# Whole-sum rows placed inside layer 0's end and between the sort's steps, and layer 0's roots by logarithm and exponential

## The chip, the core and the metric

The kernel runs on one core of a Trainium2 chip. The metric is the device time of one execution, in microseconds; lower is better. The core has five engines, each with its own queue that it works off in order: PE (TensorE, matrix products), DVE (VectorE), ACT (ScalarE), POOL (GpSimd) and SP (which here only issues transfers).

## What is computed

Four layers work on 2708 nodes with 128 features and one dense 2708 x 2708 adjacency matrix. Each has the form `x = layernorm(x + layer(x, adj))`. The change lies in layer 0's end and layer 1's beginning:

```python
# layer 0
A_hat = A + eye;  d = A_hat.sum(axis=1) ** -0.5
x = layernorm(x + (d[:, None] * A_hat * d[None, :]) @ x @ W.T + b)
# layer 1
XW = x @ W
s_col, s_row = XW @ a[0, :f], XW @ a[0, f:]
den = exp(leaky_relu(s_row[:, None] + s_col[None, :], 0.01))
num = A @ den
att = where(num != 0, den / num, 0)
x = layernorm(x + A @ (att @ XW))
```

where `layernorm(v) = (v - mean) / sqrt(var + 1e-5)`. Layers 2 and 3 (a hyperbolic layer, and one that works on the signs of the adjacency) follow and are not touched.

## The kernel before

The features lie as 128 partitions by nodes. The nodes are cut into 22 tiles of 128 (`NT`) and into six blocks of 512 columns (`NB`; the last has 148 columns). An adjacency tile `(d, c)` holds row block d and column block c, four tiles of rows by 512 columns.

**Layer 0's end.** The column blocks are finished one after the other. For a block c, `last_products` does the rest of its matrix products on PE, `summed_up` adds input and bias on DVE and squares on ACT, `norm_roots` sums the squares over the features on PE (`group_sums`, the tile `var`), takes the root on ACT, the reciprocal on DVE, and splits the result into three bf16 terms (`three_terms`, on DVE). `normed` spreads these terms over the partitions on PE (`group_spread`, the tile `rs`) and multiplies on DVE, which gives `x`. `projected` multiplies by layer 1's weights on PE, and ACT copies the outcome to `xw` and `rc` (the two scores of each node). `clamped` limits the scores (`rcl`, DVE), and `count` compares each tile of scores with 384 sample values (DVE; 44 instructions in all). The steps of neighbouring blocks are interleaved by hand. The last two blocks, 4 and 5, have no products of later blocks beside them.

**The sort.** Layer 1 needs no matrix of all pairs: the leaky exponential is a maximum of two products, so the kernel sorts the nodes by their scores into 26 groups (`GM`) and works group by group. The steps are a chain between PE and DVE: `below` (PE sums the counts), `jp` and `prev` (DVE), `prev_ps` (three transposes on PE), `prev_row` (DVE), then 26 dependent steps `jk` on DVE (L1228), each of which finds the next group's begin. Then come one-hot tables `c`, `oh`, `val` (DVE and POOL), `low` (78 small products and four larger ones on PE, L1283 and L1293, that give each node its place in its group), `pos`, `slot`, `ohs` (DVE) and two lists, `list0` and `list1` (22 products each, L1335), each read back and worked on by DVE. From the lists come the addresses of gathered adjacency rows (`row_i`, list0) and of gathered weights (`xw_i`, list1), and the exponentials `e1_l`, `e2_l`, `gj_l`. `group_matrix` (the tile `gb`) builds the first three groups' weights from `gj_l`.

**The whole sums.** The first group's numerator needs the sum of `e1 * A` over all nodes. `whole_sum(n)` does the next n of 22 rows of it (one row is one tile of 128 nodes): nine products with one output row each, on four strips of the array (L797). The rows go through the row blocks in the order 0, 4, 5, 1, 2, 3. They read adjacency tiles `kept`; those of row blocks 0 to 3 are loaded once more (the tiles B, and one in `ut`) into places that become free. When a row block's last row has been recorded, `fetch_next` records the loads into the places that it frees, in SP's queue. The finished sums are copied by ACT to `carry0` (nine copies, L1380), which lies in `xw`'s memory.

**What sets the order.** A scheduler orders the instructions of each engine by their readiness. A helper overrides it: what is recorded under `queued(ENGINE)` is issued on that engine after the last thing so recorded (`latest`), in the order of the source. Outside of it, `tc.issue_after(instruction)` sets a single edge. Before the change, the rows stand as 4 before the sort, 1 after `prev_ps`, 6 between the transposes `rb`, 3 behind them, 4 after `low`, and 4 after the last product of `list1`.

After the sort the program reads a flag and branches. In the branch POOL gathers the groups' adjacency rows (L1417), and PE starts with two `gb` and then `num` (L1461). The gathered tiles take the memory of the tiles that the whole sums read.

## Time and profile before

| | |
|---|---|
| median of 3 runs | 933.85 us (931.97 to 933.93) |
| the profiled execution | 931.1 us, of which the span from first to last instruction is 929.4 us |
| PE, DVE, ACT, POOL busy | 92%, 61%, 40%, 16% of the span |
| granted clock of TensorE, mean | 0.97 |
| layer 0's end (blocks 0 to 3) | about 124 to 163.5 us |
| its tail (blocks 4 and 5) | about 163.5 to 177 us |
| sort and lists | about 177 to 236 us |
| first `num` product in the branch | 243.77 us |

Times are microseconds from the first instruction. PE's busy share is high over the whole kernel, but it is a mean over stages: in the tail PE was busy for 4.79 of 13.5 us. So the stretch that is changed has to be read by itself, by what each engine waits for. A busy PE at half its clock also counts as busy; the clock column of the windows tells the two apart.

### The profile page before, as it was taken

The numbers are of one execution on the slowest core, as the hardware profiler recorded it, in microseconds if no ns is written. First come the engines' busy times: TensorE is split into PE (matmuls) and PEld (weight loads), VectorE is DVE, ScalarE is ACT, GpSimd is POOL, SyncE is SP. The second block draws the span as 40 slices with busy tenths as digits, with TensorE's granted clock in tenths as the row PEclk, the third lists the DMA queues.
The fourth block names the chain that finished last, engine by engine and source line by source line (L and its number), as shares of the span: only waits on it lengthen the run. The fifth ranks groups of instructions, "written<-read, shape, count | busy, mean of one in ns | idle before, by whom it ended". The sixth has DMA issues, their size and how long they took to land.

```text
span 929.4 us, 9409 instructions
## 1 busy us (share of the span) xinstructions
PE 856.4 (92%) x3268; PEld 428.0 (46%) x3268; DVE 564.3 (61%) x1221; ACT 369.6 (40%) x601; POOL 152.5 (16%) x182
## 2 busy tenths in 40 slices
PE   3799988579799999999999999989999999999997
PEld 2344534235344444444444444454344455555555
DVE  4895569898488888878786222637554464333222
ACT  3885332110677777566664111536332221000000
POOL 5321000303655554222110000000000000000000
PEclk9799999798799999999999999999999999999999
DMA  9997492195596555344431876477956293746410
GB/s 338 373 351 240 52 310 67 43 386 217 172 356 204 163 154 162 121 131 138 150 120 44 290 268 240 152 253 258 334 186 226 63 343 115 250 144 242 142 55 15
DMA packets 95834, 182.84 MB, mean 197 GB/s; under 512 B 6430, under 2 KB 23535, under 8 KB 95652
## 3 DMA queue, kind: packets, MB, share of 16 engines
q1 hardware_dynamic: 85556, 142.37, 44.5%
q0 software_dynamic: 8352, 37.76, 12.9%
q10 hardware_dynamic: 1872, 2.04, 0.6%
q8 instruction: 27, 0.44, 0.2%
q14 instruction: 27, 0.22, 0.1%
HBM read 179.33 MB, written 2.84 MB: 196 GB/s over the span
## 4 chain that ended last, share of the span: by engine, by line
PE 77%; DVE 14%; DMA 5%; ACT 2%; issue 2%; ACTq 0%; DVEq 0%
PE a L1518 21%; PE uacc L1426 14%; PE a L1797 11%; PE a L860 9%; PE num L1461 7%; PE a L1806 6%; DVE att L1474 4%; DMA A<-in_adjT_dram 4%; PE t L797 2%; DVE jk L1228 2%; DVE att L1455 2%; DMA cb<-in_adjT_dram 1%; PE pp L1755 1%; DVE counts L1041 1%; PE low L1293 1%
## 5 line engine op out<-in xcount | busy, mean ns | idle before, releaser
L1426 PE MATMUL uacc<-att,xw_g 128*128 128x512 f32 (+1 forms) x312 | 130.4, 554 | 8.9 <-DVE att L1474 8.2
L1466 ACT ACTIVATE ln<-num,inval,occ_l 128x512 f32<-128x512 f32 (+1 forms) x156 | 106.5, 722 | 65.7 <-DVE gat L1465 63.3
L1797 PE MATMUL a<-cb,ut 128*128 128x512 f32 (+2 forms) x264 | 124.8, 554 | 0.4 <-DMA cb<-in_adjT_dram 0.4
L1806 PE MATMUL a<-mask,node 128*128 128x512 f32 (+2 forms) x264 | 119.5, 534 | 0.0
L1461 PE MATMUL num<-gat,w_all 128*128 128x512 f32 (+1 forms) x276 | 114.1, 543 | 0.0
L1518 PE MATMUL a<-cb,q_b 128*128 128x512 f32 (+2 forms) x264 | 110.3, 555 | 1.7 <-DMA cb<-in_adjT_dram 1.7
L1518 PE MATMUL a<-cb,xw 128*128 128x512 f32 (+2 forms) x264 | 107.4, 550 | 0.0
L860 PE MATMUL a<-A,q_b 128*128 128x512 f32 (+2 forms) x264 | 105.8, 549 | 0.0
L1417 POOL DMA_INDIRECT gat<-in_adjT_dram,row_i x52 | 78.4, 1508 | 146.4 <-PE num L1461 79.4
L1426 PEld LDWEIGHTS uacc<-att,xw_g 128*128 128x128 f32 x312 | 55.8, 189 | 90.7 <-issue 50.0
L1465 DVE COPY gat<-num 2x512 f32<-2x512 f32 x150 | 86.0, 608 | 3.3 <-PE num L1461 3.1
L1474 DVE TENSOR_TENSOR att<-att,ln 128x1354 f32<-128x1354 f32 x52 | 81.1, 1560 | 9.6 <-ACT ln L1473 9.6
L1455 DVE TENSOR_SCALAR att<-q_b,gj_l 128x1354 f32<-128x1354 f32 x52 | 47.8, 921 | 37.8 <-PE uacc L1426 37.8
L1806 PEld LDWEIGHTS a<-mask,node 128*128 128x128 f32 (+1 forms) x264 | 47.7, 190 | 49.3 <-issue 47.5
L1461 PEld LDWEIGHTS num<-gat,w_all 128*128 128x128 f32 x276 | 51.2, 191 | 41.4 <-issue 22.7
L1473 ACT ACTIVATE ln<-ln 128x1354 f32<-128x1354 f32 x52 | 69.3, 1333 | 1.3
L1785 DVE TENSOR_SCALAR mask<-cb 128x3072 fp32r<-128x3072 f32 (+5 forms) x24 | 33.5, 1394 | 58.8 <-PE a L1806 58.6
L860 PEld LDWEIGHTS a<-A,q_b 128*128 128x128 f32 (+1 forms) x264 | 45.6, 190 | 47.9 <-issue 46.9
L1518 PEld LDWEIGHTS a<-cb,xw 128*128 128x128 f32 (+1 forms) x264 | 45.0, 190 | 46.3 <-issue 46.3
L1518 PEld LDWEIGHTS a<-cb,q_b 128*128 128x128 f32 (+1 forms) x264 | 44.6, 189 | 46.2 <-issue 42.3
L231 ACT ACTIVATE sq_l<-s 128x512 f32<-128x512 f32 (+1 forms) x11 | 6.6, 604 | 147.1 <-DVE s L1815 116.7
L1060 ACT ACTIVATE xw<-A 128x2048 f32<-128x2048 f32 (+3 forms) x36 | 57.0, 1583 | 8.2 <-issue 4.4
(446 smaller groups left out, 904.7 us busy)
## 6 DMA issues: line engine op xcount, KB each, us to landing
cb<-in_adjT_dram SPq DMA_DIRECT2D x15, 2816.0 KB
cb<-in_adjT_dram SPq DMA_DIRECT2D x15, 2560.0 KB
A<-in_adjT_dram SPq DMA_DIRECT2D x25, 1024.0 KB
B<-in_adjT_dram SPq DMA_DIRECT2D x18, 1024.0 KB
cb<-in_adjT_dram SPq DMA_DIRECT2D x3, 814.0 KB
cb<-in_adjT_dram SPq DMA_DIRECT2D x3, 740.0 KB
ut<-in_adjT_dram SPq DMA_DIRECT2D x2, 1024.0 KB
A<-in_adjT_dram SPq DMA_DIRECT2D x5, 296.0 KB
```

The lines of the kernel that those rows point to most:

```text
L860: nc.tensor.matmul(acc[c][:, :w], lhsT=z[:kw, k, :], rhs=t[:kw, i, :w], start=c not in begun, stop=(d == NB - 1 and k == NT - 1), skip_gro ...
L1417: return nc.gpsimd.indirect_dma_start(out=gat[g], out_offset=None, in_=adj_h, in_offset=bass.IndirectOffsetOnAxis(ap=row_i[:, h, g : g + 1 ...
L1426: nc.tensor.matmul(uacc[c][:, : cb - ca], lhsT=xw_g[:, g, :], rhs=att[:, ca:cb], start=(g == 0), stop=(g == GM - 1),)
L1455: nc.vector.tensor_scalar(att, q_b[:, h0 : h0 + HALF], gj_l[:, g : g + 1], 1.0, op0=ALU.mult, op1=ALU.max)
L1461: nc.tensor.matmul(num[:, : cb - ca], lhsT=(w_first if g < FIRST else w_all)[:, g, :], rhs=gat[g][:, ca:cb], start=True, stop=True)
L1465: nc.vector.tensor_copy(gat[g + 1][0:2, ca:cb], num[0:2, : cb - ca])
L1466: nc.scalar.activation(ln_n[:, ca:cb], num[:, : cb - ca], AF.Ln, scale=occ_l[:, g : g + 1], bias=inval[:, g : g + 1],)
L1473: nc.scalar.activation(ln_n, ln_n, AF.Exp, scale=-1.0)
L1474: nc.vector.tensor_mul(att, att, ln_n)
L1518: nc.tensor.matmul(acc[:, :w], lhsT=weights[:kw, k, :], rhs=pc[:kw, t, :w], start=(k == 0), stop=(k == NT - 1),)
L1797: nc.tensor.matmul(acc[:, :w], lhsT=edge[:ke, k, :], rhs=pc[:ke, t, :w], start=(k == 0), stop=False, skip_group_check=True,)
L1806: nc.tensor.matmul(acc[:, :w], lhsT=node[:kw, k, j, :], rhs=mask[:kw, t - ma, :w], start=False, stop=(k == NT - 1 and j == 1), skip_group_ ...
```

## The change

1. `norm_roots`: instead of Sqrt on ACT and a reciprocal on DVE, ACT takes the logarithm and then twice the exponential of -0.5 times it: once into bf16 (`term`, the first of the three terms) and once into fp32 (`r`). `three_terms` leaves out its first cast.
2. ACT's function table for Ln and Exp is loaded right behind the tanh of `prepare_rest`, and what is queued on ACT afterwards comes behind that load.
3. The exponentials `e1` are taken block by block in `clamped`.
4. The rows are recorded by `sum_rows` at new places: 1 after the roots of blocks 4 and 5, 1 between `normed` of block 4 and of block 5, 2 after `projected` of block 5, 3 between `below` and `prev_ps`, 6 between the `rb` as before, 3 behind them, 4 after `low` and the flag's product `gps`, and 2 ahead of `list1`. None stands behind `list1`. The products of `prev_ps`, `low`, `gps` and the lists are put into the fixed order of PE too.
5. The product of `oh` with the partition's number, twice 128 x 572 elements, moves from POOL to ACT.

```diff
--- before.py
+++ after.py
@@ -257,13 +257,14 @@
                 stop=True,
             )
 
-    def three_terms(two, r, rest, term):
+    def three_terms(two, r, rest, term, begun=False):
 
 
         n = r.shape[0]
         for i, dst in enumerate((rest, two)):
             src = rest if i else r
-            nc.vector.tensor_copy(term, src)
+            if i or not begun:
+                nc.vector.tensor_copy(term, src)
             nc.vector.scalar_tensor_tensor(dst, term, behind[:n, i : i + 1], src, op0=ALU.mult, op1=ALU.add)
 
     def group_spread(ps, two, b):
@@ -381,6 +382,8 @@
     bsum = const.tile([P, F], F32, tag="bsum", name="bsum")
     w2ext = const.tile([P, F + 1], F32, tag="w2ext", name="w2ext")
 
+    curved = []
+
     def prepare_rest():
 
         ysq = const.tile([P, F], F32, tag="ysq", name="ysq")
@@ -388,7 +391,7 @@
         nc.vector.tensor_reduce(y2, ysq, AX.X, ALU.add)
         bn = clipped_norm("bn", y2, 1)
         bt = c_tile("bt", 1)
-        nc.scalar.activation(bt, bn, AF.Tanh)
+        curved.append(nc.scalar.activation(bt, bn, AF.Tanh).ins)
         bs = multiplied("bs", divided("bq", bt, bn, 1), proj_scale("bp", bt, 1), 1)
         nc.vector.tensor_scalar(y, b2_s, bs, None, op0=ALU.mult)
         nc.vector.tensor_mul(ysq, y, y)
@@ -969,10 +972,12 @@
             r, rest = own[:, :P], own[:, P : 2 * P]
             term, two = (own[:, i * P : (i + 1) * P].bitcast(BF16)[:, :P] for i in (2, 3))
             with queued(ACT):
-                nc.scalar.activation(r, pv[:n, :P], AF.Sqrt, bias=eps_c[:n, :])
+
+                nc.scalar.activation(r, pv[:n, :P], AF.Ln, bias=eps_c[:n, :])
+                nc.scalar.activation(term, r, AF.Exp, scale=-0.5)
+                nc.scalar.activation(r, r, AF.Exp, scale=-0.5)
             with queued(DVE):
-                nc.vector.reciprocal(r, r)
-                three_terms(two, r, rest, term)
+                three_terms(two, r, rest, term, True)
             works[c, "r"] = two
 
         def normed(c):
@@ -1021,6 +1026,8 @@
                 if c == NB - 1:
                     for i in range(2):
                         nc.vector.tensor_add(cmp_v[:, i, span], cmp_v[:, i, span], pad_big[:, span])
+            with queued(ACT):
+                nc.scalar.activation(e1[:, span], rcl[:, 0, span], AF.Exp)
             if c == 0:
                 ps = ps_tile("samples_ps")
                 with queued(PE):
@@ -1047,6 +1054,10 @@
                         op1=ALU.add,
                         accum_out=counted[:, i, t + 1 : t + 2],
                     )
+
+        def sum_rows(n):
+            with queued(PE):
+                return whole_sum(n)
 
         scaled = None
 
@@ -1101,6 +1112,8 @@
                 prepare_finish()
         with tc.issue_after(scaled), tc.issue_after(rooted[0]):
             prepare_rest()
+        with tc.issue_after(curved[0]):
+            latest[ACT] = nc.scalar.preload_act_table_set("natural_log_exp_and_others").ins
         nc.sync.dma_start(out=diag_d, in_=bass.AP(tensor=adjT.tensor, offset=0, ap=[[N + 1, N], [1, 1]]))
 
         fetch_next()
@@ -1131,12 +1144,15 @@
         count(NB - 3, 1, 3)
         norm_roots(NB - 2)
         norm_roots(NB - 1)
+        sum_rows(1)
         count(NB - 3, 3, 6)
         normed(NB - 2)
+        sum_rows(1)
         normed(NB - 1)
         count(NB - 3, 6)
         projected(NB - 2)
         projected(NB - 1)
+        sum_rows(2)
         clamped(NB - 2)
         count(NB - 2)
         clamped(NB - 1)
@@ -1156,11 +1172,6 @@
 
 
         with queued(ACT):
-            nc.scalar.activation(e1[:, : tiles(1)[0]], rcl[:, 0, : tiles(1)[0]], AF.Exp)
-        with queued(PE):
-            whole_sum(4)
-        with queued(ACT):
-            nc.scalar.activation(e1[:, tiles(1)[0] :], rcl[:, 0, tiles(1)[0] :], AF.Exp)
             nc.scalar.activation(e2, rcl[:, 0, :], AF.Exp, scale=0.01)
 
         with tc.tile_pool(name="sort", bufs=1) as st_p:
@@ -1203,21 +1214,19 @@
                     )
             nc.vector.tensor_tensor(prev[:, 0, :], prev[:, 0, :], prev[:, 1, :], op=ALU.max)
             prev_ps = ps_tile("prev_ps")
-            for q in range(len(SAMPLES)):
-                turned = nc.tensor.transpose(
-                    prev_ps[:, q * P : (q + 1) * P], prev[:, 0, q : q + 1].to_broadcast([P, P]), ident
-                )
-            with tc.issue_after(turned.ins):
-                summed = whole_sum(1)
-            latest[PE] = summed.ins
+            sum_rows(3)
+            with queued(PE):
+                for q in range(len(SAMPLES)):
+                    nc.tensor.transpose(
+                        prev_ps[:, q * P : (q + 1) * P], prev[:, 0, q : q + 1].to_broadcast([P, P]), ident
+                    )
             for b in range(NB):
                 w, cs = width(b), bslice(b)
                 with queued(PE):
                     pr = bcast_block(rcl[:, 0, :], b, f"rb{b}")
                     whole_sum(1)
                 nc.scalar.activation(q_b[:, cs], pr[:, :w], AF.Exp, scale=0.99)
-            with queued(PE):
-                whole_sum(3)
+            sum_rows(3)
             prev_row = srt([P, NS], "prev_row", F16)
             nc.vector.tensor_copy(prev_row, prev_ps[:, :NS])
 
@@ -1274,32 +1283,31 @@
                 )
                 nc.vector.tensor_sub(oh[i], c3[i][:, :, :GM], c3[i][:, :, 1:])
                 nc.gpsimd.tensor_mul(val[i][:, :, 0, :], oh[i], tile_b.unsqueeze(2).to_broadcast(grid))
-                nc.gpsimd.tensor_scalar(val[i][:, :, 1, :], oh[i], part_f, None, op0=ALU.mult)
+                nc.scalar.activation(val[i][:, :, 1, :], oh[i], AF.Copy, scale=part_f)
             low = {}
             for i in range(2):
                 for h, (ta, tb) in enumerate(((0, t_a), (t_a, NT))):
                     low[i, h] = acc_tile(2 + 2 * i + h, f"low{i}_{ta}")
                     nn = (tb - ta) * GM
-                    nc.tensor.matmul(
-                        low[i, h][:, :nn],
-                        lhsT=upper,
-                        rhs=oh[i][:, ta:tb, :],
-                        start=True,
-                        stop=False,
-                        skip_group_check=True,
-                    )
-                    for t in range(tb - 1):
-                        first = max(t + 1, ta)
-                        placed = nc.tensor.matmul(
-                            low[i, h][:, (first - ta) * GM : nn],
-                            lhsT=ones_b,
-                            rhs=oh[i][:, t, :].unsqueeze(1).to_broadcast([P, tb - first, GM]),
-                            start=False,
-                            stop=(t == tb - 2),
+                    with queued(PE):
+                        nc.tensor.matmul(
+                            low[i, h][:, :nn],
+                            lhsT=upper,
+                            rhs=oh[i][:, ta:tb, :],
+                            start=True,
+                            stop=False,
                             skip_group_check=True,
                         )
-            with tc.issue_after(placed.ins):
-                summed = whole_sum(4)
+                        for t in range(tb - 1):
+                            first = max(t + 1, ta)
+                            nc.tensor.matmul(
+                                low[i, h][:, (first - ta) * GM : nn],
+                                lhsT=ones_b,
+                                rhs=oh[i][:, t, :].unsqueeze(1).to_broadcast([P, tb - first, GM]),
+                                start=False,
+                                stop=(t == tb - 2),
+                                skip_group_check=True,
+                            )
             below0 = srt([P, 1], "below0")
             okb = srt([P, 1], "okb")
             nc.vector.tensor_reduce(below0, neg_sum, AX.X, ALU.add)
@@ -1310,7 +1318,9 @@
             nc.vector.tensor_scalar(good, good, okb, None, op0=ALU.mult)
             nc.vector.tensor_reduce(gs, good, AX.X, ALU.add)
             gps = ps_tile("gps")
-            nc.tensor.matmul(gps[0:1, 0:1], lhsT=gs, rhs=ones[:, 0:1], start=True, stop=True)
+            with queued(PE):
+                nc.tensor.matmul(gps[0:1, 0:1], lhsT=gs, rhs=ones[:, 0:1], start=True, stop=True)
+            sum_rows(4)
             nc.vector.tensor_scalar(flag_i, gps[0:1, 0:1], float(N), None, op0=ALU.not_equal)
 
 
@@ -1328,11 +1338,13 @@
                 nc.vector.tensor_reduce(slot[:, i, :], pos[i], AX.X, ALU.add)
                 nc.vector.tensor_scalar(slot[:, i, :], slot[:, i, :], 2.0, None, op0=ALU.add)
                 ps = ps_tile(f"list{i}")
+                if i:
+                    sum_rows(2)
                 for t in range(NT):
                     ohs = srt([P, P], f"ohs{i}_{t}", BF16, 4, "ohs")
                     nc.vector.tensor_scalar(ohs, iota_b, slot[:, i, t : t + 1], None, op0=ALU.is_equal)
-                    with tc.issue_after(summed.ins):
-                        listed = nc.tensor.matmul(
+                    with queued(PE):
+                        nc.tensor.matmul(
                             ps[:, : 6 * GM],
                             lhsT=ohs,
                             rhs=val[i][:, t, :, :].rearrange("p n g -> p (n g)"),
@@ -1367,8 +1379,6 @@
                     nc.vector.tensor_copy(occ_l, occ)
 
                     nc.vector.tensor_scalar(inval, inval, 1.0e-18, None, op0=ALU.max)
-            with tc.issue_after(listed.ins):
-                whole_sum(4)
 
             nc.vector.tensor_scalar(sc, e1_l, -1.0, unit0[:, 0:1], op0=ALU.mult, op1=ALU.add)
             nc.vector.tensor_scalar(bi, e2_l, unit0[:, 1:2], None, op0=ALU.add)
```

On PE the same instructions stand in another order. On DVE 12 are gone (six reciprocals, six casts). On ACT two table loads go and one comes, and 12 Exp (two a block in place of each of the six roots' single Sqrt, which becomes Ln), six `e1` in place of two, and two copies. On POOL two instructions are gone. SP's queue has the same transfers in the same order.

## The prediction

> **What bounds the kernel now.** I read the chain of waits first (its stretch 160 to 245 us; the change touches nothing later), then the same stretch by windows, PE's waits, the groups and SP's queue. Chain rows are start, length, work:
>
> ```profile
> 177.02 6.72 PE t L797 x58
> 184.50 3.23 DVE jp L1195 x12
> 187.97 0.92 PE prev_ps L1207 x3
> 188.91 0.57 DVE prev_row L1222
> ...
> 216.01 4.61 PE t L797 x56
> ...
> 225.86 3.28 PE list L1335 x19
> 229.14 6.49 PE t L797 x50
> ```
>
> Three blocks of whole-sum rows (L797) lie in the open chain: 6.7, 4.6 and 6.5 us. Rows also run beside the 26 jk steps of DVE (189.5 to 206.6), where they cost nothing.
>
> ```profile
> 163.50:177.00 13.50, 4.79 (x31) 3.43 (x30) 11.93 (x43) 3.74 (x11) 3.36 (x9) 0.64 0.15 46
> 183.70:189.50 5.80, 2.13 (x16) 0.98 (x19) 4.26 (x16) 0.00 (x0) 0.00 (x0) 0.84 0.89 304
> 229.10:243.80 14.70, 8.00 (x79) 3.30 (x79) 3.82 (x18) 5.00 (x13) 6.45 (x5) 0.73 0.34 104
> ...
> 225.00:226.00 1.00, 0.28 (x2) 0.10 (x1) 1.00 (x11) 0.24 (x2) 0.00 (x0) 0.61 0.06 16
> 231.00:232.00 1.00, 1.00 (x8) 0.13 (x1) 0.00 (x0) 0.00 (x0) 0.00 (x0) 0.50 0.03 8
> ```
>
> Columns: length, busy PE, PEld, DVE, ACT, POOL, then granted clock, DMA share, GB/s. PE has idle time at layer 0's end (4.79 busy of 13.5), DVE not (11.93). The clock falls to half about 225.4, in the sparse list matmuls, and is back at 232.
>
> ```profile
> PE rs L273 <- DVE work L267: 8.7, 6, 2.5
> PE xw L993 <- DVE x L984: 1.8, 1, 1.8
> ...
> L972 ACT ACT_TABLE_LOAD x1 | 1.3, 1283 | 0.0
> ...
> L974 DVE RECIPROCAL work<-work 128x128 f32<-128x128 f32 (+1 forms) x6 | 5.7, 947 | 3.0 <-ACT work L972 3.0
> ...
> 183.34 23.06 SPq L818 DMA_DIRECT2D B<-in_adjT_dram  x12
> 206.49 2.12 SPq L818 DMA_DIRECT2D ut<-in_adjT_dram  x1
> 208.71 5.75 SPq L818 DMA_DIRECT2D B<-in_adjT_dram  x2
> ```
>
> PE waits 8.7 us for the roots' DVE chain. The B tiles' reloads are issued as rows finish and free places, and run at 386 GB/s until about 222.3.
>
> **The change part by part.** One row costs 1.18 us at full clock (four in 4.73 from 215.94), 2.38 at half (188.80 to 191.18).
>
> *Roots.* Before: Sqrt 0.37, 0.03 of handover, reciprocal 0.95, cast 0.26, first scalar_tensor_tensor: 1.61 from Sqrt's start. After: Ln 0.37, two Exp of 128x128. No such row: a 128x148 Square took 0.327, a 128x26 Exp 0.23, so 0.31 each, the second behind the first by 0.25: 1.03 from Ln's start. Below it could be 0.85 (overlapped Exps), above 1.15. DVE loses 1.2 us per block. Before's first terms began at 129.04, 138.88, 147.75, 157.39; Ln may start at 126.63 (no table load), 136.85, 145.97, 155.74, so terms at 127.66, 137.88, 147.0, 156.77: gains 1.38, 1.0, 0.75, 0.62, sum 3.75. PE's gaps ahead of rs there (1.62, 1.24, 1.00, 0.86) can hold that; ahead of PE stand its own products, so more is not to be had. e1's Exp now stands ahead of Ln on ACT and waits for DVE's rcl (133.9 to 134.05, against Ln at 136.85): hidden by the products between them.
>
> *Table loads.* The Sqrt load at 126.09 and the Exp load at 175.47 go; one load moves behind tanh, and the two degree copies queue behind it on ACT: bn 119.45, load, tanh, load to 122.45, copies to 123.6. DVE needs the first at 123.93 (PE's products end at 123.65): hidden; without PE's products it would cost 1.3. Each load was 1.28 in the trace, the next ACTIVATE 0.02 later. The Trainium skill ("ScalarE: Activation LUTs", What ACT_TABLE_LOAD costs) puts a switch at 2.66 with its drain; that speaks against two in a row: copies at 125.8, 1.9 us lost here, and 2.66 instead of 1.3 saved at the first roots, where only 0.78 lies on the path. The trace shows no such drain (Square ends 126.08, load starts 126.09): I take 1.30.
>
> *Layer 0's tail* (in before's times; shift by 3.75 afterwards). Terms of block 4 start at 165.68 (before 166.62), block 5's end at 167.7 (169.66): no reciprocals. Three counts 1.62, x of block 4, xw at 170.07 instead of 172.00. Two single rows stand ahead of rs4 and rs5: 165.2 to 166.4 (rs4 is due 166.7) and 167.3 to 168.5, rs5 then 0.7 late, but x5 is due only at 170.0: free. They read the B0 tiles, issued from 97 to 129 and landed when the DMA share fell from 1.05 to 0.34 (140 to 150): no wait; were one late, rs4 and all of DVE behind it would wait as long. They keep PE busy, so xw takes 1.7 (145 ns per matmul, as at 160.7) instead of 2.97 (250 ns). rcl4 at 171.8 instead of 174.34; the same 12 counts end at 179.4 instead of 182.05. PE's below matmuls start at 179.5 instead of 183.67, since the four d0 rows are done by 174.2. Gain 4.2.
>
> *Sort's head.* Three rows now precede prev's transposes, which need prev at 183.75 (below + 4.24, as before). PE has then idled 5.3 us and is at half clock: below to 180.1, rows 2.38 each until about 182.9, then 1.18: end 185.1, or 187.2 if all cold, 183.6 if all warm. Taken 185.1: jk at 186.35 instead of 189.50. Gain so far 3.75+3.15 = 6.9.
>
> *During jk and low.* jk is 17 us of DVE, unchanged; low starts at 201.8 (208.69-6.9). Nine rows and six rb take PE from 181.9 to about 197: hidden; without that slack they would cost 1.18 each. low cold again, 7.3, to 209.1; gps 0.2; then four rows (two d2, two d3), 4.7: list0 at 214.0 instead of 220.73. POOL's two tensor_scalars (2.28, 2.79) go to ACT, idle there for 24.5 us; a 128x572 Copy bounded by 0.60 (128x512) and 1.33 (128x1354), hidden by low. DVE's val products, 1.03 each beside POOL and 0.74 otherwise, gain 1.2, hidden by PE's rows. e1's Exps, 0.2 each, lie in ACT's idle time. flag comes earlier and nobody waits for it.
>
> *SP's queue.* Row d0's end issues B1_2 to B2_1 (5 MB) at 170.5 instead of 183.3, behind the last xw_d store; d4's end (183.8) the next 5.3 MB, d1's (194.3) the last 3.3. At 386 GB/s the first lasts to 186, the second to 199.7: never starved, so all land at 170.4+39 = 209.4 (before: 183.3 to 222.3). d3's first row is due at 211.7: no wait. d2's (194.3) meets its thin tile at 194.5.
>
> *Lists.* list0 is 3.9 us, to 217.9. Two rows now stand between the lists: 2.4 at full clock, 4.8 at half. In before the clock fell 4.7 us after the last dense row (220.7 to 225.4), which would leave these rows warm. The skill's page "TensorE: Matmul & The Clock Gate" (Part 1) has free-running windows of 3.4 us, and a mostly idle window inside list0 would make them cold; the trace's clock edges (187.7, 191.1, 208.1, 211.6) fit such windows. Between: 3.6. DVE's list0 work (1.1) hides there. list1 at 221.5, ends at 225.0 (before 229.14).
>
> *After the lists.* Before, rows 229.1 to 235.8 preceded everything: last gb at 237.73, PE's branch 5.56 (no releaser shown), num at 243.77 = list1's end + 14.6. After: list work and gj_l 1.55, gb 0.45, samples 0.46, gb2, to 2.8, branch 5.56, gb 0.5: + 8.9. The first gather waited for the last row, now at 221.5, lands 5.5 later (236.14 to 241.64) at 227.0, and ACT's nine carry copies (3.6) run beside list1: both hidden. num at 233.9 instead of 243.8: **9.9 us**.
>
> Later work hangs on PE, so this carries to the end. The profiled execution was 931.1 (span 929.4 and 1.7 around it), 2.75 under the median of the runs, 933.85. Taken from the median: 923.95, from the profiled execution 921.2.
>
> **The rivals.**
> - *All warm.* Rows after below at full clock (+1.4), low at 6.0 (+1.2), list rows 2.4 (+1.2): gain 13.7, 920.2. Against: 5.3 us of PE idleness before below; 3.4 dropped the clock at 187.7.
> - *Rows hold the sort.* All cold: 187.2 at the transposes (-2.1), 4.8 at the lists (-1.2), Ln and Exp at 1.15 (-0.5): gain 6.1, 927.8. For: the clock was at half for 3.4 us after each idle stretch.
> - *d3 late, slower.* The rows are now fixed ahead of list0 in PE's order, so a late B3 tile holds both lists. Break-even: B3's landing + 2.4+3.9+3.6+3.5+8.9 = 243.8, so 221.5; each us later costs one. At 226, 938. It needs 12 us more than the 209.4 worked out, which a starved queue could bring if d1's rows stall. Nothing in the windows (share 1.05) speaks for it.
> - *No effect.* If the branch or a gather had to wait for something I do not see, the tail's 5.7 would go, and with cold rows nothing measurable is left: 933.
>
> **How the numbers follow.** 0.2% (1.9 us) is about what can be told from no change. Forecast (gain 7.5 to 12) 0.58, all warm 0.15, rows hold 0.19, no effect 0.04, slower 0.04. Time 924.0. The range 920.0 to 929.0 leaves out the two last, half of the all-warm case and the worst of the third. Faster 0.92, same 0.04, slower 0.04.
>
> **What would show it.** Right: no table load ahead of the first Ln, Ln to terms about 1.03, PE's wait for rs near 5, jk starting at 182 to 183, list0 at 213 to 215, no row after list1, num at about 234. Wrong: DMA waits on t rows, prev_ps starting over 2 us after prev, over 4 us between the lists, or more than 6 us of PE idle ahead of the first gb in the branch.

## The result and the profile after

The changed kernel took 922.7 us (median of 4 runs, 920.86 to 923.13) where the kernel before took 933.43 beside it (4 runs, 931.97 to 933.93): 0.9884 of it, 95% interval 0.9866 to 0.9902, a gain of 10.7 us. The prediction was 924.0 us, 9.9 us gained. The profiled execution took 920.86 (span 919.1); that of before 931.1.

The chain of waits in the changed kernel, around the branch (start, length, work). The last `gb` ahead of the branch used to end at 237.73, `num` started at 243.77:

```profile
226.38 0.34 PE gb L707
...
227.61 0.47 ACT samples L708
228.07 3.47 issue
231.54 0.66 PE gb L707 x2
232.20 2.84 PE num L1471 x4
```

No row (L800) is left behind list 1, and PE's stop at the branch (the idle time between the last `gb` ahead of it and the first behind it), taken at 5.56 us from the trace of before, is shorter too: 3.97. PE's waits, first the stop in before, then the changed kernel in 123 to 240 us (total, times, longest):

```profile
PE gb L704 <- issue: 5.6, 1, 5.6
```

```profile
PE below L1187 <- DVE counts L1048: 4.6, 1, 4.6
PE low L1293 <- DVE val L1284: 4.2, 1, 4.2
PE gb L707 <- issue: 4.0, 1, 4.0
...
PE rs L274 <- DVE work L268: 1.6, 5, 0.4
...
PE t L800 <- DMA B<-in_adjT_dram: 0.7, 2, 0.5
```

The wait for the roots (`rs`) fell from 8.7 to 1.6. PE instead idles ahead of `below` and of `low`: DVE is what those stages wait for. Rows waited 0.7 us for tiles. What the two idle stretches do to the clock is in the windows (length, busy PE, PEld, DVE, ACT, POOL, granted clock, DMA share, GB/s):

```profile
157.50:170.50 13.00, 10.45 (x114) 6.10 (x117) 12.17 (x47) 5.27 (x21) 2.81 (x6) 1.00 0.14 42
176.50:182.80 6.30, 6.30 (x68) 2.81 (x69) 4.02 (x15) 0.13 (x1) 1.25 (x5) 0.75 1.05 386
206.00:207.00 1.00, 1.00 (x19) 1.00 (x18) 1.00 (x2) 0.00 (x0) 0.00 (x0) 0.51 1.00 373
218.60:221.00 2.40, 2.40 (x37) 0.93 (x36) 2.10 (x17) 0.47 (x3) 0.00 (x0) 1.00 0.01 3
224.80:232.00 7.20, 1.21 (x6) 0.81 (x7) 3.68 (x16) 2.42 (x5) 4.83 (x4) 0.69 0.50 173
```

Layer 0's end (first line) now keeps PE busy for 10.45 of 13 us at full clock. The three rows ahead of prev's transposes (second) ran at half clock for 3.2 of their 5.2 us, and `low` (third) for its first 5 us; the two rows between the lists (fourth) ran at full clock. The last line is the stretch of the branch. The Exps of the roots and SP's queue stand as forecast: 0.31 us each, and the B tiles issued from 170.67 without a gap.

```profile
L977 ACT ACTIVATE work<-work 128x128 bf16<-128x128 f32 (+1 forms) x6 | 1.9, 310 | 0.2
L978 ACT ACTIVATE work<-work 128x128 f32<-128x128 f32 (+1 forms) x6 | 1.9, 309 | 0.2
```

```profile
170.67 23.52 SPq L821 DMA_DIRECT2D B<-in_adjT_dram  x12
194.29 1.65 SPq L821 DMA_DIRECT2D ut<-in_adjT_dram  x1
196.03 5.76 SPq L821 DMA_DIRECT2D B<-in_adjT_dram  x2
```

### The profile page after: what moved, and what is told of

The parts are those of the page before. It is cut to its first block, busy times and chain, and to the rows that moved or that the text cites. A ratio compares the mean times of both kernels' runs of the same rounds, so it can differ in the third digit from the quotient of the medians.

```text
span 919.1 us, 9408 instructions
## 1 busy us (share of the span) xinstructions
PE 855.1 (93%) x3268; PEld 428.0 (47%) x3268; DVE 556.7 (61%) x1209; ACT 373.9 (41%) x618; POOL 149.0 (16%) x180
## 4 chain that ended last, share of the span: by engine, by line
PE 64%; DVE 8%; issue 1%; ACT 1%; ACTq 0%
PE a L1528 22%; PE uacc L1436 14%; PE a L1807 11%; PE num L1471 7%; PE a L1816 6%; DVE att L1484 4%; DVE att L1465 2%; PE pp L1765 1%; PE mx L1635 1%; PE su L252 1%; PE st_l L252 0%; PE gb L707 0%; ACT ln L1476 0%; PE pr_l L274 0%; ACT ln L1483 0%
```

## A table to read the experiments by

Executions of one kernel beside each other differ by 1.7 to 6.5 us, and the profiles show where part of it lies. On PE all kernels here have the same work ahead of block 0's first `var` in layer 0, yet that matmul starts at 126.1 to 130.3 us in the 14 profiles. The work from the first `num` to the issue of the last store but one is the same as well, and takes 671.5 to 675.5. So the table gives, from each kernel's one profile, the starts of `below`, list 0 and `num` counted from that `var`, three distances (`prev_ps` behind `below`, `low` to `gps`, `num` to that store), and beside them the medians of 4 to 6 timed runs with the ratio to before.

The runs fall into five groups, each beside its own runs of before. The medians of before were 933.43 beside the changed kernel, 933.14 beside again, rows_last, prev_early and jk_rows, 933.5 beside roots_only, packed, pool_val and gather_late, 934.8 beside tail_rows, gather_dep and copies_late, and 933.98 beside gather_mid. Across groups it is the ratios that compare, not the medians.

| kernel | below | prev_ps behind below | low lasts to gps | list 0 | num | num to last store but one | median us | ratio, 95% interval |
|---|---|---|---|---|---|---|---|---|
| before | 57.54 | 4.30 | 11.77 (4 rows in it) | 94.60 | 117.64 | 672.53 | 933.43 | |
| changed | 48.86 | 6.08 | 8.23 | 88.32 | 105.28 | 674.03 | 922.70 | 0.9884 (0.9866 to 0.9902) |
| again | 48.85 | 7.12 | 8.67 | 89.79 | 107.43 | 672.70 | 921.84 | 0.9871 (0.9852 to 0.9890) |
| roots_only | 49.78 | 4.40 | 12.03 (4 rows in it) | 86.84 | 109.76 | 673.23 | 928.62 | 0.9941 (0.9924 to 0.9958) |
| rows_last | 48.86 | 6.62 | 8.44 | 86.74 | 109.40 | 672.97 | 926.10 | 0.9920 (0.9904 to 0.9937) |
| prev_early | 48.85 | 4.54 | 5.88 | 85.84 | 102.90 | 675.52 | 921.20 | 0.9867 (0.9847 to 0.9887) |
| jk_rows | 48.86 | 6.66 | 5.88 | 85.46 | 103.52 | 672.40 | 919.38 | 0.9856 (0.9834 to 0.9877) |
| packed | 48.86 | 4.53 | 5.89 | 82.62 | 105.48 | 673.78 | 921.26 | 0.9862 (0.9839 to 0.9885) |
| tail_rows | 48.77 | 4.40 | 5.88 | 86.12 | 105.46 | 674.00 | 921.31 | 0.9850 (0.9828 to 0.9871) |
| pool_val | 48.86 | 7.25 | 7.15 | 88.41 | 105.83 | 671.47 | 922.13 | 0.9878 (0.9857 to 0.9898) |
| gather_late | 48.85 | 7.18 | 8.69 | 89.88 | 106.65 | 673.33 | 923.20 | 0.9883 (0.9864 to 0.9902) |
| gather_dep | 48.85 | 6.48 | 8.37 | 88.84 | 108.53 | 673.35 | 925.68 | 0.9913 (0.9896 to 0.9931) |
| gather_mid | 48.85 | 5.62 | 7.97 | 87.59 | 106.98 | 673.22 | 925.59 | 0.9910 (0.9886 to 0.9935) |
| copies_late | 48.85 | 6.93 | 8.57 | 89.50 | 106.27 | 674.41 | 923.83 | 0.9887 (0.9866 to 0.9907) |

## The experiments

In the kernel lines below, `...` stands for lines between, and the comments are not the kernel's.

**The changed kernel again** (no edit).

> The changed kernel once more, nothing edited, to see what of its profile is the same in every execution. In the first profile the gain against before is 12.3 us at layer 3's cb issues (728.35 against 740.61) and 10.3 at the end; the missing 2 us go while PE runs at half clock at layer 3's begin (clock 0.64 in 742.7 to 747.7). Theory (the loss is a chance of where the clock's windows fall): the times before layer 3 agree within 0.3 us, and layer 3's begin and the end differ by up to 2 us between executions. Rival (the loss belongs to the order of PE's work there, a mask that is made late by DVE): the same 2 us are lost again, at the same place.

Measured: 921.84. The first clause fell: block 0's `var` comes 1.5 later and the stretch to `num` is 2.15 longer than in the first profile (1.0 of it ahead of `prev_ps`, where the three rows took 6.2 us instead of 5.2, and 0.4 in a colder `low`). But the loss at layer 3's begin did not repeat: from the first `cb` issue behind that of `diag_d` to the last `cb` issue ahead of the next `diag_d` (736.51 to 761.23 in the first profile) it was 22.65 us, against 24.72 in the first profile and 22.42 in before. The windows from PE's wait on, first the changed kernel's first profile, then this one:

```profile
737.70:742.70 5.00, 3.55 (x10) 1.68 (x10) 4.51 (x6) 1.35 (x3) 0.00 (x0) 0.68 1.04 387
742.70:747.70 5.00, 5.00 (x19) 2.46 (x17) 2.25 (x6) 1.33 (x3) 0.19 (x1) 0.64 1.04 373
```

```profile
741.30:746.30 5.00, 3.64 (x9) 1.69 (x10) 4.44 (x7) 0.72 (x2) 0.00 (x0) 0.66 1.04 387
746.30:751.30 5.00, 5.00 (x23) 2.53 (x21) 2.90 (x7) 1.96 (x4) 0.19 (x1) 0.99 1.05 373
```

The same kernel with the same work has half clock for a second stretch in one execution (0.64) and not in the other (0.99). Over these 14 profiles this step takes 21.9 to 24.7. The 2 us belong to the execution, not to the change.

**Roots alone**: the kernel before with the new roots; rows, `e1` and `val` as before.

```
-                nc.scalar.activation(r, pv[:n, :P], AF.Sqrt, bias=eps_c[:n, :])
-                nc.vector.reciprocal(r, r)
+                nc.scalar.activation(r, pv[:n, :P], AF.Ln, bias=eps_c[:n, :])
+                nc.scalar.activation(term, r, AF.Exp, scale=-0.5)
+                nc.scalar.activation(r, r, AF.Exp, scale=-0.5)
...
+        with tc.issue_after(curved[0]):
+            latest[ACT] = nc.scalar.preload_act_table_set("natural_log_exp_and_others").ins
```

> The kernel before with the roots by Ln and two Exps alone (table load behind tanh, first term already begun); rows, their order, e1 and val as before. Theory (the roots gave 3.5 us of layer 0's end and the rest came from rows): PE's rs waits fall from 8.7 to under 3, block 4's var is 3.5 earlier, xw of the last blocks 4 us earlier, jk starts 3.5 to 4 earlier, and the end is 3.5 earlier than before: 929.6. Rival 1 (roots and rows need each other: with rows still queued behind the counts PE is cold at xw and below, so that the gain at var is kept but not more): the same at var, end 3.0 to 3.5. Rival 2 (layer 0's gain is lost at the rows that follow the lists): end within 1 us of before, 932.5.

Measured: 928.62, 4.9 us less than before (0.9941; the interval is 3.9 to 7.1 us). At `below` the gain is 57.54 - 49.78 = 7.8 of the whole change's 8.7, twice what was expected, and all of it still stands at `num` (7.9 in the profile; that execution lay about 2 us under its median). PE's waits:

```profile
PE rs L274 <- DVE work L268: 3.3, 6, 1.6
...
PE below L1182 <- DVE counts L1045: 0.8, 1, 0.8
```

`below` waits for DVE, no longer for the rows queued ahead of it. In before DVE's counts ended at 182.05, 55.9 behind the `var`, and the rows held `below` until 183.67: 6.1 of the 7.8 us come from DVE, which has lost the reciprocals of all six blocks, and 1.6 from the rows that now end before its counts. That the reciprocals are what DVE gained by is argued from the edit: it takes nothing else from DVE but six casts. The expectation had 3.5 us at block 4's `var` and almost nothing behind it.

**The last four rows back behind list 1.**

```
-            sum_rows(4)      # ahead of list 0
+            sum_rows(2)
-                if i:
-                    sum_rows(2)
+            sum_rows(4)      # behind list 1
```

> The four last whole-sum rows (two ahead of list 0, two between the lists) go back behind list 1, where they stood before the change. Theory (rows behind the lists cost their full length, and the first gather, which waits for the last row, falls into the stretch that PE's branch needs): list 0 starts at 212.7 instead of 215.0, list 1 ends at 220.1, rows to 224.9 or later, gather lands at 230.5, PE's gap at the branch is 5.6 us again instead of 4.0, num at list 1's end + 14.6 = 234.7 instead of 232.0, the end 2.7 later: about 925.4. Rival 1 (only the sum of rows counts, their place does not): rows 4.7 at full clock behind list 1 cover the 1.6 us in which PE waits for gj_l, the branch stays at 4.0, num at 231.0 to 231.5, the end 0.5 to 1 earlier: about 922. Rival 2 (the clock falls in the lists and the rows run at half, as in the kernel before): rows 6.5, num 236 or later, about 927.

Measured: 926.1, 4.3 above the changed kernel run beside it: not rival 1, and between the theory (925.4) and rival 2 (927). List 0 came earlier (86.74) as it should, but the rows behind list 1 took 6.2 us (half clock for part of it), which is rival 2's 6.5, and list 1 waited 0.25 and 0.72 for DVE's work on list 0, which the rows between had covered. PE's stop was 5.49 again. `num` at 109.40 is where the roots alone had put it (109.76). By the profiles, then, only these four rows' moves pay; what the others gain at `below` (0.9) is lost ahead of prev. The runs leave room for more: five of the six runs of rows_last lie under all six of roots_only, and the medians are 926.1 and 928.6, though the intervals of the two ratios overlap. Whether the other moves bring up to 2 us is open.

**Two of three rows moved behind prev's transposes.**

```
-            sum_rows(3)
+            sum_rows(1)
             with queued(PE):    # prev's transposes
+            sum_rows(2)
```

> Of the three rows that stand ahead of prev's transposes on PE, two are moved behind them. In the changed kernel prev is ready at 179.87 and its transposes start at 181.66, behind rows. Theory (these rows hold the sort): transposes at 179.95, first jk at 181.1 instead of 182.8, everything behind it 1.7 earlier, list 0 at 213.3, end 1.7 earlier: 921.0. Rival (the gain is given back): the fifth block's rows end 1 us later, so the last B tiles are issued and land later than 209.9, and the rows ahead of list 0 wait for them: list 0 at 214.3 or later, end within 0.8 us of the changed kernel.

Measured: 921.2, not told apart from the changed kernel (921.84) by the runs. In the profile the hold is gone:

```profile
181.92 0.54 PE L1220 MATMUL prev_ps<-ident,prev 128*128 128x128 f32 x3 [1.21 <-DVE prev L1215]
...
212.84 0.45 PE L800 MATMUL t<-B,e 128*1 128x160 f32 x8 [0.44 <-DMA B<-in_adjT_dram]
213.72 0.72 PE L800 MATMUL t<-B,e 128*1 128x148 f32 x12 [0.44 <-DMA B<-in_adjT_dram]
```

PE now waits for prev (1.21), the transposes come 4.54 behind `below` instead of 6.1 to 7.2, and `low` is warm (5.88). The rival is right in part: the rows ahead of list 0 wait twice for tiles (the last two lines). `num` at 102.90 is the earliest of all, but this execution lost 2 to 3 us behind it (675.52), and the median shows no gain; what the other executions lost there is not known.

**Two more rows inside the jk steps.**

```
-            sum_rows(3)      # behind the last rb
+            sum_rows(5)
-            sum_rows(4)      # behind gps
+            sum_rows(2)
```

> Two more rows run inside the jk steps (five instead of three behind the last rb) and two fewer between low and list 0. In the changed kernel PE idles 4.2 us ahead of low, low then takes 8.2 us (clock 0.51 in 206 to 207), and four rows, 4.75 us, stand between low and list 0. Theory (PE's idle stretch hides the two rows, and shortened to about 1.8 us it leaves the clock high): low 202.0 to 208.3, two rows from 209.9 when the last B tiles have landed, list 0 at 212.4 instead of 215.0: end 2.6 earlier, 920.1. Rival 1 (clock falls all the same): low ends at 210.2 as now, list 0 at 212.7: 2.3 earlier. Rival 2 (the rows wait for the third block's tiles and hold low): low starts later than 202.0, and the gain is under 1 us.

Measured: 919.38, the lowest median: 2.5 under the changed kernel run beside it, four of its five runs under all five of that one (the intervals of the two ratios overlap, and tail_rows below has the same ratio). The rows are hidden, `low` is warm:

```profile
203.47 0.38 PE L1293 MATMUL low<-val,upper 128*128 128x494 bf16 x1 [3.18 <-DVE val L1284]
...
213.05 0.45 PE L1347 MATMUL list<-val,ohs 128*128 128x156 bf16 x4
214.36 3.00 PE L1347 MATMUL list<-val,ohs 128*128 128x156 bf16 x18 [0.85 <-DVE ohs L1345]
```

List 0 at 85.46 against 88.32 to 89.88 in three profiles of the changed kernel's order: 2.9 to 4.4 earlier, where the theory had 2.6. DVE is next: list 0 waits 0.85 for it.

**Both moves, and all four last rows between the lists**: `sum_rows(1)`, transposes, `sum_rows(2)`; 5 rows in the jk steps, none ahead of list 0, 4 between.

> The two moves that gained, together, and one more: two of the three rows behind prev's transposes, five rows inside the jk steps, none between low and list 0, four between the lists. In the run with early transposes the rows ahead of list 0 waited twice 0.44 us for the last B tiles, and with five rows in the jk steps list 0 started at 212.2 on the changed kernel's clock. Theory (rows ahead of list 0 hold it, and between the lists they stand beside DVE's work on list 0): jk at 181.2, low warm from 200.4 to 206.3, list 0 at 208.6 when DVE's slots are ready, four rows from 212.2 to 217.0 without waiting, list 1 to 220.8 instead of 224.8: num 4.0 us earlier than in the changed kernel run beside it, 917.5 to 918. Rival 1 (B tiles late or rows at half clock between the lists): rows take 7 to 9.5, list 1 ends at 223 to 225.5, no gain over five rows in the jk steps (919.4). Rival 2 (DVE is the next bound: val, pos and slot end at 210): list 0 at 210.3, gain 2.5, 919.3.

Measured: 921.26; rival 1, with help of rival 2. List 0 starts at 82.62, but DVE feeds it slowly, PE is mostly idle, and the clock falls for the rows behind it:

```profile
209.89 0.73 PE L1347 MATMUL list<-val,ohs 128*128 128x156 bf16 x4 [1.46 <-DVE ohs L1345]
...
215.00:219.00 4.00, 4.00 (x21) 0.69 (x24) 2.26 (x18) 0.34 (x2) 0.00 (x0) 0.50 0.03 8
```

Four rows took 6.7 us, at least 4 of these us at half clock: in the profile `num` is no earlier than in the changed kernel.

**Three rows ahead of below**: 3 rows behind `clamped` of the last block, 1 ahead of prev's transposes, 3 in the jk steps, 2 ahead of list 0, 3 between the lists.

> Three of the fifth block's rows run in PE's idle stretch of 4.6 us ahead of below, one ahead of prev's transposes, six with the rb's and three behind them, two ahead of list 0 and three between the lists. Theory (nothing holds prev, the B tiles are asked for no later than in the changed kernel, low is warm, and only one row ahead of list 0 needs the last tiles): on the changed kernel's clock jk at 181.1, low 200.3 to 206.2, list 0 at 210.9 to 211.5, list 1 ends at 222 instead of 224.8: num 2.8 earlier, 919.0. Rival 1 (rows between list 0 and list 1 at half clock, as with four of them): list 1 ends at 224, 921. Rival 2 (rows of the fifth block hold below or xw): below later than 175.6, and the gain is lost there.

Measured: 921.31, and since before ran at 934.8 beside it, a ratio of 0.9850, like that of jk_rows (0.9856). Nothing holds `below` or prev, `low` is warm, but the second row ahead of list 0 needs the last tiles and waited 1.65 and 0.54 us for them, and the rows between the lists began at half clock: list 0 at 86.12, `num` at 105.46. So the profile shows rival 1 in part, and a wait for tiles that the expectation had not; the ratio is nearer to the theory. The last tiles' landing is a floor under every order that puts a row of theirs ahead of list 0.

**The val scalings back on POOL.**

```
-                nc.scalar.activation(val[i][:, :, 1, :], oh[i], AF.Copy, scale=part_f)
+                nc.gpsimd.tensor_scalar(val[i][:, :, 1, :], oh[i], part_f, None, op0=ALU.mult)
```

> The changed kernel with the two scalings of val back on POOL instead of ACT. Theory (hidden, as the prediction has it): POOL takes 2.3 and 2.8 us for them and DVE's val products go from 0.74 back to 1.03 beside POOL, 1.2 us of DVE, hidden behind low and the four rows ahead of list 0: list 0 and the end within 0.3 us of the changed kernel run beside it. Rival (with low's end earlier DVE's slots are what list 0 waits for): list 0 up to 1.2 later, 923.0.

Measured: 922.13, list 0 at 88.41, `num` at 105.83: inside the spread of the changed kernel's profiles. This part of the change brings nothing that can be seen.

**Why PE's stop at the branch is shorter.** First the gathers' row numbers were computed behind list 1.

> The changed kernel with the row numbers of the gathers worked out only behind list 1, so that gather 0 starts at 226.4 instead of 221.3; PE's order is untouched. Theory (PE's stop at the branch is longer when the gathers' rows are read in the same stretch, 5.6 in the kernel before and 5.5 with the rows behind the lists, against 4.0 to 4.3 where gather 0 had landed before): the stop is 5.5, num 36 quarters of a microsecond less exactly 1.3 to 1.5 us later, the end 1.4 later. Rival (the stop depends on the whole-sum rows just ahead of it, or on chance): the stop stays 3.8 to 4.3; then num waits for gather 0 (landing 231.9, first rows copied to 232.8), 0.8 later at most.

The edit didn't bring that about: gather 0 started 0.33 us behind list 1's first matmul, as in the changed kernel. (Of the expectation's clause on `num` only "1.3 to 1.5 us later" is meant.) The run (923.2, stop 3.80) is a third look at the changed kernel and tells nothing on the theory. Then the numbers were made to depend on list 1's last result, so that they can't be early:

```
+                    nc.vector.scalar_tensor_tensor(at, inval, 0.0, node0, op0=ALU.mult, op1=ALU.add)
...
+                        nc.vector.tensor_scalar(fi, at, 2.0, float(h), op0=ALU.mult, op1=ALU.add)
```

> The changed kernel with the gathers' row numbers made to depend on list 1's last result (one more 128x26 DVE operation), which the earlier attempt had not brought about: there gather 0 still started 0.3 us behind list 1's first matmul. Now it can start only about 1.8 us behind list 1's end, in the stretch of the branch, as in the kernel before. Theory (the stop at PE's branch is longer when the gathers move their rows in the same stretch: 5.4 to 5.6 in the three runs with rows behind the lists, 3.8 to 4.3 in the others): the stop is 5.4 to 5.6 and num comes 1.5 later. Rival 1 (the stop is longer where ACT's nine carry copies still run behind the last gb: they end 2.5 to 2.6 us ahead of PE's next gb in the runs with the long stop): the stop is 3.8 to 4.3, and num waits for gather 0 alone, 0.5 to 1.5 later. Rival 2 (whole-sum rows just ahead of the branch do it): as rival 1.

The stop was 3.86, against the theory as it stood; `num` waited 2.63 for gather 0's rows instead. Next, ACT's copies alone:

```
...
-            for c, a, b, o, bank, at in sums_of:
-                nc.scalar.copy(carry0[0:1, c * BW + a : c * BW + b], tot[bank][o : o + 1, at : at + b - a])
+            with queued(ACT):
+                for c, a, b, o, bank, at in sums_of:
+                    nc.scalar.copy(carry0[0:1, c * BW + a : c * BW + b], tot[bank][o : o + 1, at : at + b - a])
```

> The changed kernel with ACT's nine carry copies behind the samples instead of beside list 1: they start where the last samples end and take 3.0 to 3.6; gather 0 stays early. Theory (gathers beside the branch lengthen the stop): the stop of PE at the branch stays 3.8 to 4.3. Rival 1 (ACT's late copies lengthen it): PE's next gb comes 2.5 us behind the last copy, a stop of 5.5 to 6.2. In both, num waits for the carry's copy by DVE, which waits for the last of these copies: num 0.5 to 2 later than in the changed kernel.

The stop was 3.81 with the copies (3.6 us) behind the samples: they are not the cause. (`num`, which was expected later, came at 106.27, within the 105.28 to 107.43 of the changed kernel's order.) In gather_dep, though, gather 0 was issued only 0.16 us behind the last `gb`, and moved almost nothing yet in the two us that followed. So once more, with the numbers hung on list 1's first copy (`occ` in place of `inval`):

> As the last attempt with the gathers' row numbers, but made to depend on list 1's first copy instead of its last result, so that gather 0 starts about 1.6 to 2.0 us ahead of the end of the last gb in front of PE's branch, as it did in the kernel before (1.6 ahead). In the last attempt it started 0.16 behind that end, the stop was 3.86, and the DMA engines were still almost idle (share 0.05 to 0.13) in the two us that followed; in the three runs with the long stop their share was 0.5 to 1.2 there. Theory (gathers' data in the first two us of the stop lengthen it): the stop is 5.4 to 5.6. Rival (whole-sum rows directly ahead of the branch lengthen it, whatever the gathers do): the stop stays at 3.7 to 4.3, with the DMA engines as busy as in the long ones. Num waits for gather 0 or for PE, 1.5 to 2.5 later than in the changed kernel, the end 1.5 to 2.5 later.

Here gather 0 was issued 1.33 us ahead of the end of that `gb`, and the stop was 5.76. The `gb` behind the branch, and the two us behind the last `gb` ahead of it, in gather_dep and then in gather_mid:

```profile
232.58 0.66 PE L707 MATMUL gb<-ident,gj_l 128*128 128x128 f32 x2 [3.86 <-issue]
...
228.72:230.72 2.00, 0.00 (x1) 0.00 (x0) 0.00 (x0) 0.46 (x1) 1.54 (x2) 0.52 0.06 16
```

```profile
235.94 0.66 PE L707 MATMUL gb<-ident,gj_l 128*128 128x128 f32 x2 [5.76 <-issue]
...
230.20:232.20 2.00, 0.00 (x0) 0.00 (x0) 0.27 (x2) 0.46 (x1) 1.50 (x2) 0.50 0.71 138
```

DMA share 0.06 and a stop of 3.86; 0.71 and 5.76, with no row behind list 1 in either: the time of the gathers is what the two kernels differ in. From list 1's end to `num` both took longer than the 7.1 to 7.9 us of the changed kernel's order, 9.96 and 9.66.

The share of the first two us does not order the stops, though: in the changed kernel it was 0.42 with a stop of 3.97. The traces show what the stop ends with. The profile lists a DMA queue of the kind `instruction` (packets, MB, share):

```profile
q8 instruction: 27, 0.44, 0.2%
```

These are 27 packets of 16384 bytes. In the changed kernel PE begins some 200 to 340 matmuls and weight loads from one packet to the next, but only 10 between one that starts inside the stop and the next. In all 14 traces PE's first matmul behind the branch comes 1.4 to 1.7 us behind the end of the one inside the stop. That one starts 1.15 to 1.7 us behind the last `gb` in the ten short stops (3.65 to 4.30), 2.9 to 3.3 in the four long ones (5.44 to 5.76, among them before with 3.08). Up to its start the DMA engines' share was 0.02 to 0.40 in the short stops and 0.81 to 0.95 in the long ones. So PE most likely waits for its next instructions, and gathers that move rows just then delay them. That the packet queues behind these rows is argued: no trace shows when it was asked for.

## Why the prediction was right

The total and the mechanisms were right, but several terms were off and made each other good, so that the total came within 1 us is in part luck. Against the working, the first profile has `below` 0.8 us earlier, the lists 1.5 and the stretch behind them 1.7 shorter, but the sort's head 0.5 and `low` 0.9 longer: `num` 2.5 earlier than worked out. Behind `num` 1.5 of it was lost.

*Roots.* Ln's start to the first terms took 1.08 us (predicted 1.03). At `var` of block 4 the profile shows 2.94 gained by the clock, 3.46 if the 0.52 is taken off by which this execution was late before the change begins (predicted 3.75). With the tail, `below` is 8.7 earlier (predicted 3.75 + 4.17 = 7.9). Roots alone give 7.8 of that, so most of the tail's gain comes with the last two blocks' reciprocals, and the rows moved inside it bring 0.9 (`xw` at 1.61 us instead of 2.97, as predicted). PE's wait for `rs`, predicted near 5, fell to 1.6: with roots alone it is 3.3, and the single rows ahead of the last two `rs` can fill the rest.

*Table loads.* Tanh's load, tanh and the second load stand at 120.16, 121.45 and 121.67; both loads took 1.28, with 0.02 between load and activation. The copies end at 124.04, and nothing waited. The switch of 2.66 us with a drain, which the Trainium skill ("ScalarE: Activation LUTs", What ACT_TABLE_LOAD costs) names and which the prediction set aside, did not show.

*Sort's head.* The step was right in kind and too small: a hold of 185.1 - 183.75 = 1.35 was taken with the rows partly warm, 5.0 us for three. It was 1.8 in the first profile (6.08 - 4.30), where the rows took 5.2 and began 0.3 later behind `below`, and 2.8 and 2.9 in the other two of the same order (again, gather_late), where they were nearly all cold: 6.2. That is past the 2 us which the prediction had named as a sign of being wrong. This is the rival "rows hold the sort", true in this place; prev_early removes it.

*Low.* Predicted 7.3 again; 8.2 to 8.7. PE's idle stretch ahead of it grew (4.2 to 5.0 us), and the rows hidden in the jk steps left room for two more.

*SP's queue.* Predicted: all tiles landed at 209.4, no wait for the last tiles' rows. So it was: the DMA share fell from 1.07 to 0.45 in 209 to 210. (The 39 us are those of before's trace, which moved 364 GB/s in them; the three parts that the prediction names, 13.6 MB at 386 GB/s, add up to 35.) The 0.7 us of waits lie inside the jk steps, where PE had 4.2 us to spare. Rows that were moved nearer to that time did wait (prev_early, tail_rows), which shows how little room there was.

*Lists.* Rows between them 3.6 predicted, 2.44 measured: at full clock, the all-warm case. List 0 was taken at 3.9 us, which in before's trace is a group of 24 products, two of them list 1's; list 0's own 22 took 3.5 there and 3.5 here.

*After the lists.* 8.9 us predicted from list 1's end to `num`, 7.2 measured. The term that was off is PE's branch, taken as a fixed 5.56 and worth 3.65 to 4.3 where no gather fills the DMA engines ahead of the packet that ends it. The prediction had seen that the gather comes 14.6 us earlier, but only asked whether its landing is hidden.

*To the end.* Gained at `num`: 117.64 - 105.28 = 12.4 in the first profile, 10.2 and 11.0 in the other two of the same order; at the end 10.7, 11.3 and 10.3 by the medians. "This carries to the end" holds on average; a single profile loses or wins up to 2 us behind `num`, of which the clock at layer 3's begin is the part that was looked at.

## What to carry to other kernels

Rows put into another engine's shadow pay twice where they keep TensorE's clock up, and cost up to double where they start it cold on the open path: two rows more in the jk steps brought list 0 forward by 2.9 us or more and the median by 2.5 (not clear of its interval), three rows ahead of three small transposes held these by 1.8 to 2.9. Before a stop is taken as a constant, look at what the DMA engines carry during it. And when executions scatter as much as the effect, time the stretch from its own first instruction to its own last in the profile, beside the medians.

## What the hardware showed

- PE's stop at the branch was 3.65 to 4.3 us with the DMA engines' share at 0.02 to 0.40 until a 16 KB packet of the queue `q8 instruction` started, 5.4 to 5.8 with gathers' rows there and a share of 0.81 to 0.95. It ended 1.4 to 1.7 us behind that packet's end in all 14 profiles. DVE's stop was 3.2 to 3.5 in all of them.
- The same idle stretch did not always cost the same: behind 4.6 us of waiting `below` ran at full clock in the first profile (0.32 us) and at half in the next (0.48), and the three rows behind it took 5.2 and 6.2 us. Nor does its length decide: `low` was warm behind 1.9 to 3.2 us of idleness in three kernels and lost part of its clock behind 2.5 and 3.0 in roots_only and before.
- What decides can be worked out from the traces. The granted clock changes only at distances that are multiples of 3.41 us, and where this grid lies differs from one execution to the next. Of the windows of this grid at full clock between 125 and 240 us of the 14 profiles, 331 in all, 287 were followed by full clock: PE was busy for at least 44% of each. 44 were followed by half clock: PE was busy for at most 43% of 36 of them, and the other 8 begin in the stretch of the lists; why these differ is not shown. Ahead of `low`, before's idle stretch fell into one window (first line, busy for 28%, and the second shows the clock behind it), that of jk_rows was split over two (46 and 60%), and the clock stayed:

```profile
204.74:208.15 3.41, 0.95 (x18) 0.43 (x10) 3.30 (x10) 0.00 (x0) 0.00 (x0) 1.00 1.07 366
208.15:211.56 3.41, 2.87 (x9) 1.30 (x9) 3.41 (x7) 0.00 (x0) 2.84 (x2) 0.50 1.05 386
```

```profile
198.71:202.13 3.42, 1.58 (x44) 1.11 (x37) 3.26 (x11) 0.00 (x0) 0.00 (x0) 1.00 1.06 390
202.13:205.54 3.41, 2.06 (x17) 1.40 (x17) 3.41 (x7) 1.44 (x2) 2.04 (x2) 1.00 1.03 380
205.54:208.95 3.41, 3.41 (x60) 2.75 (x58) 3.41 (x6) 0.00 (x0) 0.95 (x1) 1.00 1.05 387
```

- With the same instructions, layer 3's begin took 21.9 to 24.7 us in 14 profiles, and block 0's `var` came at 126.7 to 130.3 in the 13 profiles that share the new table load.
